# Layer-0 q, k and v projections as reduced-precision matmuls on whole-number weights, with the scales applied to the sums

## The chip, the cores and the metric
One core of one Trainium2 chip runs the kernel. The metric is the device time of one execution in microseconds (us). Engines: PE (TensorE, matmuls), DVE (VectorE), ACT (ScalarE), POOL (GpSimd) and SP (SyncE, here only a queue that issues transfers; ACT and POOL issue transfers too). Each engine and each queue takes its instructions in the order in which the program holds them.

## The reference, cut to what matters
Two transformer layers on 1024 tokens of width 512. The change lies in the attention of layer 0, with 32 query heads and 8 key/value heads of width 128 and 4-bit weights:
```python
w = (qw.astype(jnp.float32) - 8.0) * jnp.repeat(scales, 128, axis=0)   # a scale per 128 rows and column
q, k, v = h @ w_q, h @ w_k, h @ w_v            # h: normalised tokens, 1024 x 512
q, k = q*cos + rotate_half(q)*sin, k*cos + rotate_half(k)*sin
scores = where(causal, q @ k.T / sqrt(128), min)  # 4 query heads share one k and v
ctx = softmax(scores) @ v
x = x + ga * (ctx @ w_o)                       # w_o dequantised like w_q
```
`rotate_half` exchanges the two halves of a head's 128 columns and negates one. A feed-forward layer, a second attention and a second feed-forward layer follow; they are not touched.

## The kernel before
Tokens are held transposed: `hT[half]` has 512 tokens in the free dimension and the 512 features as `NC` = 4 chunks of 128 partitions. A prologue loads, normalises and transposes the tokens and projects the first head group. Then come 8 head groups `g` (one k/v head and its `REP` = 4 query heads each) of 8 steps; a step handles 128 query rows `qi` in the order 3, 7, 2, 6, 1, 5, 0, 4. Steps with `qi` of 4 and more are called long here, the others short. `tc.manual_schedule()` keeps each engine's instructions in the order in which the code writes them, so the loop body is the schedule.

A step works in four slices `s` of 32 query rows (times four heads, so 128 rows of scores):
- `scores(u, s)`: one or two matmuls (L331) into a score tile of two PSUM banks, pool `sp` with three tiles; DVE masks (L335, L337) and takes the maximum (L339); ACT takes the exponential with the row sum (L341) into `pr`.
- `normalize(u, s)`: DVE's reciprocal (L348), ACT's product with it in place (L350).
- `turn_probs(u, b)`: DVE transposes 32x32 blocks (L355), and four transfers (L357) carry the result into `pT`, from SP for even `b` and from POOL for odd `b`. Block 0 is turned at the end of its own step, blocks 1 to 3 in the next.
- `context(old)` (L366): the product of `pT` of two steps ago with v, one matmul for each of its `qi` + 1 blocks, copied out by ACT (L372). `project_o(old)` (L377): four matmuls with the dequantised output weights. `residual`: DVE multiplies by the gate (L385), POOL adds to `x` (L386).

Beside that each step of groups 0 to 6 does some `piece()`s of the next group's projections. `project_rope` runs four float32 matmuls (L219) of 512 columns that accumulate over the chunks in one PSUM bank, DVE multiplies by the cosine (L225) and, half by half with the partitions exchanged, by the sine (L227, L228), and POOL adds both into `kT` or `qT` (L232). `project_v` (L299) does v for two heads in every second group, evicted by `evict` in turn on ACT and DVE. The matmul results of all of these come from one PSUM pool `psA[0]` (tag "mm") of two banks, which `context` and `project_o` use as well. `exchange()` turns weights that have landed into floats (`ready`, DVE's L212; k also by ACT's L276) and loads the next (`load`: the int32 weights and, spread over 128 partitions, their scales). `plan(g, i)` says by hand which weights and pieces belong to which step. The last group has no projections (`last_group_step`).

Of the kernel before, what the change touches and what calls it, by code (L numbers as in the profile page):

```python
# [9 lines left out]
F32 = mybir.dt.float32  # L10
I32 = mybir.dt.int32
# [6 lines left out]
P = 128  # L18
# [24 lines left out]
def block_kernel(ctx: ExitStack, tc: tile.TileContext, a: dict, out: bass.AP):  # L43
# [66 lines left out]
    mod = {}  # L110

# [41 lines left out]
    def gate_row(l, j, bank, spread=None):  # L153

        spread = gate_spread(l, j) if spread is None else spread
        ps = bank()
        for c in range(NC):
            nc.tensor.transpose(ps[:, bass.ts(c, P)], spread[:, c, :], ident)
        g = const.tile([P, D], F32, tag=f"gate{j}", name=f"gate{j}")
        evict(g, ps)  # L160
        mod[l, j] = g
# [25 lines left out]
    with ExitStack() as st:  # L187
        wp = st.enter_context(tc.tile_pool(name="a0w", bufs=3))
        kvp = st.enter_context(tc.tile_pool(name="a0kv", bufs=2))
        rp = st.enter_context(tc.tile_pool(name="a0r", bufs=2))  # L190
        qp = st.enter_context(tc.tile_pool(name="a0q", bufs=2))
        ordered = st.enter_context(tc.manual_schedule())
        psA[0] = st.enter_context(tc.tile_pool(name="psA0", bufs=2, space=PSUM))
        first = st.enter_context(ExitStack())
        fp = first.enter_context(tc.tile_pool(name="m0s", bufs=1))
        tmp_open(first, "m0", bufs=9, wm=4)
        trp = first.enter_context(tc.tile_pool(name="psM0", bufs=4, space=PSUM))
        psA[1] = first.enter_context(tc.tile_pool(name="psM1", bufs=2, space=PSUM))
# [12 lines left out]
        def dequant(dst, q, s):  # L211
            nc.vector.scalar_tensor_tensor(dst, q, -ZERO, s, ALU.add, ALU.mult)  # L212

        def project_rope(dst, wf, halves):

            for half in halves:
                ps = psum_mm()
                for c in range(NC):
                    nc.tensor.matmul(  # L219
                        ps, lhsT=wf[:, c, :], rhs=hT[half][:, c, :],  # L220
                        start=(c == 0), stop=(c == NC - 1),
                    )
                sl = bass.ts(half, 512)
                t1 = rp.tile([P, 512], F32, tag="t1", name="t1")
                nc.vector.tensor_mul(t1, ps, cosT[:, sl])  # L225
                t2 = rp.tile([P, 512], F32, tag="t2", name="t2")
                nc.vector.tensor_mul(t2[0:64, :], ps[64:128, :], sinT[64:128, sl])  # L227
                nc.vector.tensor_mul(t2[64:128, :], ps[0:64, :], sinT[0:64, sl])  # L228
                if len(dst.shape) == 3:
                    t1, t2 = (t.rearrange("p (b i) -> p b i", i=B) for t in (t1, t2))  # L230
                    sl = bass.ts(half, 512 // B)
                nc.gpsimd.tensor_tensor(dst[:, sl], t1, t2, ALU.add)  # L232

        raw, wf = {}, {}
        kT, vv, qT, wo, vs_ = {}, {}, {}, {}, {}

        def load(kind, *n):

            if kind == "m":
                raw[kind, *n] = mod_load(*n)  # L240
                return
            shape = [P, NC, P] if kind in "qk" else [P, 2, 2 * HD] if kind == "v" else [P, D]
            wi = wp.tile(shape, I32, tag="wi", name="wi")
            ws = wp.tile(shape, F32, tag="ws", name="ws")
            if kind in "qk":
                wsrc, ssrc = a[f"qw_{kind}"][n[0]], a[f"s_{kind}"][n[0]]
            elif kind == "v":
                sl = slice(2 * n[1], 2 * n[1] + 2)
                wsrc, ssrc = a["qw_v"][n[0] // 2][:, sl, :], a["s_v"][n[0] // 2][sl, :]
            else:  # L250
                h = n[0] * REP + n[1]
                wsrc, ssrc = a["qw_o"][h * P : (h + 1) * P, :], a["s_o"][h]
            nc.sync.dma_start(wi, wsrc)
            nc.sync.dma_start(ws, ssrc.partition_broadcast(P))
            raw[kind, *n] = wi, ws

        def ready(kind, *n):

            if kind == "m":
                mod_sum(*n, raw.pop((kind, *n)))  # L260
                return
            wi, ws = raw.pop((kind, *n))
            if kind in "qk":
                dst = wp.tile([P, NC, P], F32, tag="wf", name="wf", bufs=2)
                wf[kind, n[0]] = dst
            elif kind == "v":
                if n[1] == 0:
                    vs_[n[0]] = wp.tile([P, NC, 2 * HD], F32, tag="vf", name="vf", bufs=1)
                dst = vs_[n[0]][:, 2 * n[1] : 2 * n[1] + 2, :]
            else:  # L270
                if n[1] == 0:
                    wo[n[0]] = wp.tile([P, REP, D], F32, tag="wo", name="wo", bufs=2)
                dst = wo[n[0]][:, n[1], :]
            dequant(dst, wi, ws)
            if kind == "k":
                nc.scalar.mul(dst, dst, SC0)  # L276

        def project_k(g, half):
            if half == 0:
                kT[g] = kvp.tile([P, S], F32, tag="kT", name="kT")  # L280
            project_rope(kT[g], wf["k", g], (half,))

        def project_q(h, half):

            g, r = divmod(h, REP)
            if (r, half) == (0, 0):
                qT[g] = qp.tile([P, S // B, REP, B], F32, tag="qT", name="qT")
            project_rope(qT[g][:, :, r, :], wf["q", h], (half,))

        def project_v(g, ts):  # L290

            if ts[0] == 0:
                v = kvp.tile([P, NT, 2 * HD], F32, tag="v", name="v")
                vs_[g, "v"] = v
                vv[g], vv[g + 1] = v[:, :, :HD], v[:, :, HD:]
            for t in ts:
                ps = psum_mm()
                for c in range(NC):
                    nc.tensor.matmul(  # L299
                        ps[:, : 2 * HD], lhsT=tok(hT, c, t), rhs=vs_[g][:, c, :],  # L300
                        start=(c == 0), stop=(c == NC - 1),
                    )
                evict(vs_[g, "v"][:, t, :], ps[:, : 2 * HD])
# [84 lines left out]
        def plan(g, i):  # L388


            n, h0 = g + 1, (g + 1) * REP
            if g + 1 == NKV:
                parts = [("m", 1, j, c) for j in (3, 4, 5) for c in range(NC)]
                return parts[2 * i - 2 : 2 * i] if i else [], parts[2 * i : 2 * i + 2], []
            m = (0, 3 + g) if g < 3 else (1, g - 4) if g > 3 else None
            m = [("m", *m, c) for c in range(NC)] if m else []
            v = [("v", n, 0), ("v", n, 1)] if n % 2 == 0 else []
            q = [("q", h0 + r) for r in range(REP)]
            o = [("o", n, r) for r in range(REP)]
            k = [("k", n + 1)] if n + 1 < NKV else []  # L400
            ks = [lambda s=s: project_k(n, s) for s in range(2)]
            qs = [[lambda r=r, s=s: project_q(h0 + r, s) for s in range(2)] for r in range(REP)]
            vp = [lambda t=t: project_v(n, (t, t + 1)) for t in range(0, NT, 2)] if v else []
            if g == 0 and i < 7:
                o0 = [("o", 0, r) for r in range(REP)]
                return (
                    (q[:1], o0[1:2], ks),
                    (q[1:2] + o0[:2], o0[2:] + q[2:3], qs[0]),
                    (o0[2:], q[3:] + o[:1], qs[1]),
                    (q[2:] + o[:1], o[1:], []),  # L410
                    (o[1:], m[:2], qs[2]),
                    (m[:2], m[2:], []),
                    (m[2:], k, qs[3]),
                )[i]
            return (
                ([], o[:1], ks),
                (q[:2], v, []),
                (o[:1] + v, q[2:] + o[1:2], qs[0] + qs[1]),
                (q[2:] + o[1:2], o[2:], []),
                (o[2:], m[:2], qs[2] + vp[:2]),  # L420
                (m[:2], m[2:], []),
                (m[2:], k, qs[3] + vp[2:]),
                (k, [("q", h0 + REP + r) for r in range(2)] if k else [], []),
            )[i]

        hT = [keep.tile([P, NC, 512], F32, tag=f"h{i}", name=f"hT{i}") for i in range(2)]
# [39 lines left out]
        def ln_evict(half, banks):  # L468
            shift, scale1 = mod[0, 0], mod[0, 1]
            for c in range(NC):  # L470
                h = hT[half][:, c, :]
                if c % 2:
                    nc.scalar.activation(
                        h, banks[c], AF.Identity,
                        bias=shift[:, c : c + 1], scale=scale1[:, c : c + 1],
                    )
                else:
                    nc.vector.tensor_scalar(
                        h, banks[c], scale1[:, c : c + 1], shift[:, c : c + 1],
                        ALU.mult, ALU.add,  # L480
                    )
# [27 lines left out]
        ready("k", 0)  # L509
        ln_evict(0, banks)  # L510
        load_tables(0)
        load("v", 0, 0)
        load("v", 0, 1)
# [1062 lines left out]
```

## Time and profile before
| what | value |
|---|---|
| median of 3 timed runs | 1839.43 us (1837.96 to 1839.64) |
| span of the profiled execution | 1835.6 us, 23046 instructions |
| prologue: first L219 matmul to first score matmul | 19.3 to 69.3 us |
| head groups 0 to 6 | 69.3 to 980.0 us |
| last head group | 980.0 to 1095 us |
| everything after layer 0's attention | 1095 to 1835.6 us |
| memory traffic | 74.90 MB read, 2.36 MB written |

The span goes from the first to the last instruction on the chip, the timed runs have a little more around it. Times in views of the trace are microseconds from the span's start. A line such as `L219 PE MATMUL mm<-hT,wf 128*128 128x512 f32 x8` names the line of the kernel, the engine, the operation, the tile written and the tiles read, the shape and how many such instructions were merged; what stands in brackets behind it is the idle time before it and what released it. A float32 matmul leaves two records. Matmuls are pipelined, so that the pitch from start to start says what one costs, not its duration. Line numbers are those of the kernel that a trace or a sentence speaks of.

### The profile page before, as it was taken

What the parts mean: (1) busy time and instruction counts of PE and PEld (TensorE: products, weight loads), DVE (VectorE), ACT (ScalarE), POOL (GpSimd) and SP (SyncE); (2) the same over time, 40 slices, a digit from 0 to 9 for tenths busy, and PEclk for the clock granted to TensorE, in tenths of its full rate; (3) what the DMA queues carried; (4) which work ended last, traced back from release to release, by engine and by line L of the source; (5) the groups of instructions that cost most, each with busy time, mean ns of one, the idle gap of its engine ahead of it and who ended that gap; (6) DMA issues with size and microseconds to landing.
All of it is one profiled execution on the core that took longest, in us unless ns stands there. A gap on an engine that the chain in (4) does not pass through costs nothing.

```text
span 1835.6 us, 23046 instructions
## 1 busy us (share of the span) xinstructions
PE 1786.1 (97%) x6818; PEld 842.1 (46%) x6818; DVE 1164.5 (63%) x2824; ACT 671.4 (37%) x1401; POOL 486.8 (27%) x712
## 2 busy tenths in 40 slices
PE   7999999999999999999999999999999999999999
PEld 4444445444455444455444444444544443333444
DVE  6778675676765777766777764232455678677543
ACT  1143433434434434333345530000114345355631
POOL 1335443444433444434444430001110100200000
PEclk9999999999999999999999999999999999999999
DMA  6164552354543554534544553001000002000000
GB/s 234 57 168 123 133 149 74 105 149 114 137 115 82 127 130 115 149 95 112 122 119 128 149 154 136 1 0 52 1 1 5 8 8 78 4 5 8 8 18 34
DMA packets 87739, 156.40 MB, mean 85 GB/s; under 512 B 25264, under 2 KB 33072, under 8 KB 87616
## 3 DMA queue, kind: packets, MB, share of 16 engines
q1 hardware_dynamic: 70064, 117.00, 22.2%
q0 software_dynamic: 17312, 37.54, 8.5%
q8 instruction: 55, 0.90, 0.2%
q14 instruction: 68, 0.56, 0.1%
q10 hardware_dynamic: 240, 0.41, 0.1%
HBM read 74.90 MB, written 2.36 MB: 42 GB/s over the span
## 4 chain that ended last, share of the span: by engine, by line
PE 73%; DVE 15%; ACT 5%; issue 4%; DMA 2%; SPq 0%; POOL 0%; ACTq 0%; DVEq 0%; POOLq 0%
PE mm L366 10%; PE sc L852 8%; PE sc L331 8%; PE mm L219 8%; PE mm L377 7%; PE sc L1117 6%; PE sc L1070 5%; PE sc L886 4%; PE ctx L1169 4%; DVE pr L355 3%; PE mm L299 3%; PE sc L973 2%; ACT pr L341 2%; ACT pr L350 2%; DVE nb L339 2%
## 5 line engine op out<-in xcount | busy, mean ns | idle before, releaser
L341 ACT ACTIVATE pr<-sc,nb 128x512 f32<-128x512 f32 (+7 forms) x256 | 189.3, 740 | 502.3 <-DVE nb L339 390.6
L219 PE MATMUL mm<-hT,wf 128*128 128x512 f32 x640 | 289.8, 597 | 7.4 <-DVE t L228 3.7
L357 POOL DMA_DIRECT2D pT<-pr x509 | 251.0, 499 | 141.2 <-DMA pT<-pr 41.2
L331 PE MATMUL sc<-kT,qT 128*128 128x512 f32 (+15 forms) x768 | 263.5, 466 | 2.9 <-ACT pr L341 2.9
L366 PE MATMUL mm<-pT,v 128*128 128x512 f32 x576 | 258.7, 594 | 2.0 <-DVE gu L585 1.6
L377 PE MATMUL mm<-wo,ctxT 128*128 128x512 f32 x512 | 232.9, 597 | 7.4 <-DVE wo L212 3.5
L355 DVE STREAM_TRANSPOSE pr<-pr 128x512 f32<-128x512 f32 (+7 forms) x256 | 189.3, 760 | 80.0 <-ACT pr L350 72.5
L331 PEld LDWEIGHTS sc<-kT,qT 128*128 128x128 f32 x768 | 141.9, 191 | 160.2 <-issue 143.6
L1117 PE MATMUL sc<-q,kv 32*128 32x512 f32 (+3 forms) x768 | 194.0, 542 | 3.6 <-DVE mx L1085 2.0
L350 ACT ACTIVATE pr<-pr,rs 128x512 f32<-128x512 f32 (+7 forms) x256 | 190.9, 765 | 8.9 <-DVE rs L348 8.9
L339 DVE TENSOR_REDUCE nb<-sc 128x1 f32<-128x416 f32 (+31 forms) x256 | 181.1, 708 | 8.8
L1133 ACT ACTIVATE pspace<-sc 128x512 f32<-128x512 f32 (+3 forms) x303 | 131.5, 493 | 147.1 <-PE sc L1126 108.1
L219 PEld LDWEIGHTS mm<-hT,wf 128*128 128x128 f32 x640 | 118.4, 190 | 143.7 <-issue 119.1
L1070 PE MATMUL sc<-kv,q 32*128 32x512 f32 (+3 forms) x768 | 174.6, 532 | 3.7 <-DVE mx L1085 1.4
L386 POOL TENSOR_TENSOR x<-x,ot 128x512 f32<-128x512 f32 x62 | 78.4, 1265 | 348.2 <-DVE ot L385 268.5
L366 PEld LDWEIGHTS mm<-pT,v 128*128 128x128 f32 x576 | 107.7, 190 | 121.1 <-issue 113.1
L852 PE MATMUL sc<-hT,gu 128*128 128x512 f32 x352 | 153.3, 594 | 0.9 <-DVE ot L385 0.9
L1080 DVE CUSTOM_DVE_ANT_0 q<-sc,cwide 128x128 f32<-128x128 f32 (+3 forms) x256 | 125.5, 490 | 42.7 <-PE sc L1070 17.6
L377 PEld LDWEIGHTS mm<-wo,ctxT 128*128 128x128 f32 x512 | 96.2, 191 | 115.4 <-issue 100.4
L232 POOL TENSOR_TENSOR qT<-t,t 128x512 f32<-128x512 f32 x64 | 86.5, 1352 | 113.1 <-DVE t L228 112.8
L852 PEld LDWEIGHTS sc<-hT,gu 128*128 128x128 f32 x352 | 66.1, 190 | 86.4 <-issue 81.6
L1117 PEld LDWEIGHTS sc<-q,kv 32*128 32x128 f32 x768 | 71.4, 186 | 71.8 <-ACT pspace L1133 23.3
(199 smaller groups left out, 1849.9 us busy)
## 6 DMA issues: line engine op xcount, KB each, us to landing
wm<-in_wmodT_dram SPq DMA_DIRECT2D x44, 256.0 KB
wi<-in_qw_q_dram SPq DMA_DIRECT2D x32, 256.0 KB
ws<-in_s_q_dram SPq DMA_DIRECT2D x32, 256.0 KB
wi<-in_qw_o_dram SPq DMA_DIRECT2D x32, 256.0 KB
ws<-in_s_o_dram SPq DMA_DIRECT2D x32, 256.0 KB
pT<-pr SPq DMA_DIRECT2D x64, 128.0 KB
pT<-pr POOLq DMA_DIRECT2D x64, 128.0 KB, 3.3
pT<-pr SPq DMA_DIRECT2D x64, 112.0 KB
```

Source lines behind the costliest of these rows:

```text
L219: nc.tensor.matmul(ps, lhsT=wf[:, c, :], rhs=hT[half][:, c, :], start=(c == 0), stop=(c == NC - 1),)
L331: nc.tensor.matmul(ps[:, n0 : n0 + w], lhsT=q, rhs=kT[u.g][:, n0 : n0 + w], start=True, stop=True)
L339: nc.vector.tensor_reduce(nb, ps[:, : d0 + B], AX.X, ALU.max, negate=True)
L341: nc.scalar.activation(u.pr[:, :, :, s, :].rearrange("p j k i -> p k j i"), ps[:, :nk].rearrange("p (k j i) -> p k j i", j=NB, i=B), AF.Ex ...
L350: nc.scalar.activation(pr, pr, AF.Copy, scale=u.rs[s])
L355: nc.vector.transpose(t, t)
L357: queues[(REP * b + r) % len(queues)].dma_start(u.pT[b * B : (b + 1) * B, r, :, :, :].rearrange("p k s i -> p (k s i)"), t[r * B : (r + 1) ...
L366: nc.tensor.matmul(ps, lhsT=vv[u.g][:, kj, :], rhs=u.pT[:, :, kj, :, :], start=(kj == 0), stop=(kj == u.n - 1),)
L377: nc.tensor.matmul(ps, lhsT=u.ctxT[:, r, :], rhs=wo[u.g][:, r, :], start=(r == 0), stop=(r == REP - 1),)
L852: nc.tensor.matmul(ps, lhsT=w[:, m, c, :], rhs=hTc[b][:, c, :], start=(c == 0), stop=(c == NC - 1),)
L1070: nc.tensor.matmul(ps[:, at : at + w], lhsT=u.q[kp, bass.ts(i, P)], rhs=kT1[kp, u.g, n0 : n0 + w], start=True, stop=True,)
L1117: nc.tensor.matmul(ps[:, : QW - q0], lhsT=kT1[kp, u.g, bass.ts(kb, P)], rhs=u.q[kp, q0:QW], start=True, stop=kb < 4 * u.Q,)
```

## The change
The projections of q, k and v are written anew, and the loop around them with it.
- The tokens are kept as two float32r tiles, `hi` (the value as float32r holds it) and `lo` (the rest), made from each transposed bank by one ACT and two DVE instructions.
- Weights of q, k and v become whole numbers in float32r by one ACT instruction (`ready`); their scales are no longer spread over the partitions but stand as one column per head and chunk in `scol`, loaded once. The output weights are dequantised by ACT and POOL.
- One half of one head is a `Job`. `sums`: per chunk two matmuls (`lo`, `hi`) into a bank of its own, so four banks a job; chunks 0 and 2 are evicted with their scale by ACT, chunks 1 and 3 added with theirs by DVE; POOL adds the two partial sums. `swap`: two transfers exchange the halves of the 128 partitions into `r`, on SP (in the prologue on ACT's queue). `end`: POOL multiplies by the cosine (in the prologue DVE), DVE `r` by the sine, POOL adds. For v, `end` transposes on PE and copies out by ACT, so v is projected for one head in every group.
- The PSUM pool of the matmuls has four banks instead of two, that of the score tiles two tiles instead of three.
- In groups 0 to 6 three of four blocks of `turn_probs` go out on SP (`wide`). Short steps open two jobs, long steps one. The hand-written `plan` becomes a table by place, and `exchange` loads whatever fits next.
- `gates[5] = big` places one gate tile in another pool.

```diff
-        psA[0] = st.enter_context(tc.tile_pool(name="psA0", bufs=2, space=PSUM))
+        psA[0] = st.enter_context(tc.tile_pool(name="psA0", bufs=4, space=PSUM))
...
-            dequant(dst, wi, ws)
-            if kind == "k":
-                nc.scalar.mul(dst, dst, SC0)
+                nc.scalar.add(dst, wi, -ZERO)
+                nc.gpsimd.tensor_tensor(dst, dst, ws, ALU.mult)
+                return
...
+            nc.scalar.add(dst, raw.pop((kind, *n)), -ZERO)
+            wf[kind, n[0]] = dst
...
+            def sums(self):
+
+                w, at = wf[self.kind, self.n], place[self.kind] + self.n
+                self.y = y = rp.tile([P, 512], F32, tag="ya", name="ya")
+                z = rp.tile([P, 512], F32, tag="yb", name="yb", bufs=1)
                 for c in range(NC):
-                    nc.tensor.matmul(
-                        ps[:, : 2 * HD], lhsT=tok(hT, c, t), rhs=vs_[g][:, c, :],
-                        start=(c == 0), stop=(c == NC - 1),
+                    ps = psum_mm()
+                    for part in (lo, hi):
+                        nc.tensor.matmul(
+                            ps, lhsT=w[:, c, :], rhs=part[self.half][:, c, :],
+                            start=part is lo, stop=part is hi,
+                        )
+                    dst, s = (y, z)[c // 2], scol[:, at, c : c + 1]
+                    if c % 2 == 0:
+                        nc.scalar.activation(dst, ps, AF.Copy, scale=s)
+                    else:
+                        nc.vector.scalar_tensor_tensor(dst, ps, s, dst, ALU.mult, ALU.add)
+                nc.gpsimd.tensor_tensor(y, y, z, ALU.add)
+
+            def swap(self):
+
+                self.swapped = True
+                if self.kind == "v":
+                    return
+                self.r = rp.tile([P, 512], F32, tag="yr", name="yr")
+                q = nc.scalar if self.early else nc.sync
+                q.dma_start(self.r[0:64, :], self.y[64:128, :])
+                q.dma_start(self.r[64:128, :], self.y[0:64, :])
...
+                first = nc.vector if self.early else nc.gpsimd
+                first.tensor_tensor(y, y, cosT[:, sl], ALU.mult)
+                nc.vector.tensor_mul(self.r, self.r, sinT[:, sl])
+                nc.gpsimd.tensor_tensor(dst, t1, t2, ALU.add)
...
-        sp = st.enter_context(tc.tile_pool(name="a0s", bufs=3, space=PSUM))
+        sp = st.enter_context(tc.tile_pool(name="a0s", bufs=2, space=PSUM))
...
+        wide = [nc.sync] * 3 * REP + [nc.gpsimd] * REP
...
                 scores(u, 0)
...
+                turn_prev(1)
+                close_job()
+                if qi < NT // 2:
+                    open_job()
+                    scores(u, 1)
+                    turn_prev(2)
+                    normalize(u, 0)
+                    turn_prev(3)
+                    swap()
                     if old:
                         context(old)
+                    scores(u, 2)
+                    normalize(u, 1)
+                    close_job()
+                    open_job()
+                    scores(u, 3)
+                    normalize(u, 2)
+                    exchange(g, i)
+                    swap()
+                else:
+                    scores(u, 1)
...
+                    normalize(u, 0)
+                    turn_prev(2)
+                    turn_prev(3)
+                    open_job()
+                    if old:
+                        context(old)
+                    swap()
+                    scores(u, 2)
+                    normalize(u, 1)
+                    exchange(g, i)
+                    scores(u, 3)
+                    normalize(u, 2)
+                    close_job()
+                assert not waiting
                 if old:
                     ps = project_o(old)
+                normalize(u, 3)
...
+                for b in range(2 if (g, i) == (NKV - 2, NT - 1) else 1):
+                    turn_probs(u, b, wide)
                 if old:
                     residual(old, ps)
```
`open_job` starts the next waiting job, `swap` issues the transfers of the oldest job that has none yet, `close_job` ends the oldest job that has been swapped.

## The prediction
> **What bounds the kernel now.** I read the page first: TensorE (PE) is the only engine near its limit.
> ```profile
> PE 1786.1 (97%) x6818; PEld 842.1 (46%) x6818; DVE 1164.5 (63%) x2824; ACT 671.4 (37%) x1401; POOL 486.8 (27%) x712
> ```
> Then busy time by stretch, cut where the first score matmul of each head group starts. Columns: length, then busy time of PE, weight load, DVE, ACT, POOL, then granted clock and DMA.
> ```profile
> 593.30:717.00 123.70, 122.94 (x313) 57.50 (x312) 89.11 (x207) 52.28 (x107) 54.89 (x82) 1.00 0.49 124
> 717.00:856.10 139.10, 137.07 (x378) 69.39 (x377) 93.49 (x213) 53.74 (x111) 54.88 (x82) 1.00 0.44 118
> ```
> PE has under 2.1 us idle in a group. Groups that also project v take 139.1, the others 123.7; the six full ones average 131.5. DVE is already at two thirds. From 1095 us on nothing changes.
>
> Third, one long step (group 5, qi 7), engine by engine, since the change moves work from PE to DVE, ACT, POOL and the queues. PE, each record half of one float32 matmul:
> ```profile
> 731.39 3.33 PE L331 MATMUL sc<-kT,qT 128*128 128x512 f32 x8
> 734.55 4.46 PE L366 MATMUL mm<-pT,v 128*128 128x512 f32 x10
> 738.85 3.54 PE L331 MATMUL sc<-kT,qT 128*128 128x512 f32 x8
> 742.23 3.60 PE L377 MATMUL mm<-wo,ctxT 128*128 128x512 f32 x8
> ```
> Start to start: five context matmuls take 4.30 (0.86 each), two score slices 3.38, the output projection 3.43. DVE of that step, with its end:
> ```profile
> 733.67 0.14 DVE L335 MEMSET sc<- 128x96 f32 x1
> ...
> 735.12 0.70 DVE L355 STREAM_TRANSPOSE pr<-pr 128x512 f32<-128x512 f32 x1
> ...
> 747.84 1.25 DVE L355 STREAM_TRANSPOSE pr<-pr 128x1024 f32<-128x1024 f32 x1 [1.91 <-ACT pr L350]
> 749.01 0.65 DVE L385 TENSOR_TENSOR ot<-mm,gate 128x512 f32<-128x512 f32 x1
> 749.68 0.14 DVE L335 MEMSET sc<- 128x96 f32 x1
> ```
> One slice costs DVE 1.45 (memset, mask, max). DVE starts the step's first slice 2.3 us after PE began it, and the next step's 4.0 after (749.68 against 745.66). DVE's round is 16.0 us where PE's is 14.3: already longer, and only PE's long projections let DVE catch up. ACT:
> ```profile
> 742.40 1.11 ACT L341 ACTIVATE pr<-sc,nb 128x1024 f32<-128x1024 f32 x1 [2.22 <-PE sc L331]
> ...
> 743.50 1.14 ACT L350 ACTIVATE pr<-pr,rs 128x1024 f32<-128x1024 f32 x1
> 744.54 1.10 ACT L341 ACTIVATE pr<-sc,nb 128x1024 f32<-128x1024 f32 x1
> ```
> An exponential with its read-back takes 1.10, a normalisation 1.04.
>
> **What PE is spared.** A q or k half costs 4 x 0.86 = 3.45, a v head the same. A job is now 8 float32r matmuls of 512 columns, of which the trace has none. The nearest row is v's, whose records also last half of a 512-column record's pitch:
> ```profile
> 22.81 7.07 PE L299 MATMUL mm<-vf,hT 128*128 128x256 f32 x32
> ```
> 29.71 - 22.81 over 32 is 0.216 us each. Bounds: 0.129 (bf16, 128 columns: 33.0 us over 256) and 0.43 (a whole float32 record). I take 0.216, so 1.73 per job. The Trainium skill, FP8 and Floating Point Precision, TensorE Precision Notes, gives four passes for float32 and truncation to a shorter format for the reduced read; one pass of four would make a job 1.72. No run so far shows it. Per group: minus 11 x 3.45, plus 12 x 1.73, plus 8 transposes at 0.11: 131.5 becomes 115.2. If PE stayed the bound, 7 x 16.3 = 114 us would be gained.
>
> **Where it goes instead.** The matmul banks are now a ring of four, and one job fills all four. In a long step PE's order is score slices 0 and 1, the job, context. The context takes the bank of the job's first chunk, so it waits for ACT's scaled eviction of that chunk (`sums`), and ACT's order puts that behind exponential 1 and normalisation 0. In the program of after this wait stands on the first context matmul of every long step. So DVE's round becomes one serial chain. Long step qi 7: slice 0 1.45, transpose 0.71, the sine product of the job before 0.69 (as L225 and L227), slice 1 1.45, exp 1.10, normalise 1.04, eviction 0.65 (between 0.58 of the context copy L372 and 0.77 of L473), context 4.30, score slice 2 1.69, its DVE part 1.45, exp 1.10, normalise 1.04, ACT's dequantisation 0.63 (L276), exp 1.10, two normalisations 2.08, transpose 1.17, residual product 0.67; six crossings between engines 0.5. Sum 22.8. The same with the shorter rows and other contexts: qi 6 25.0 (context of 8 blocks, three dequantisations), qi 5 22.0, qi 4 20.2; together 90.0.
>
> Short step qi 3: slice 0 0.9; the first two chunks wait for exp 0.68 and eviction 0.65: 2.3; two DVE evictions 1.37, slice 1 0.9, two transposes and a reciprocal 1.8: 6.4. Meanwhile the SyncE queue, which now carries 12 probability transfers a step instead of 8, and at 0.63 us each, sends four after the second transpose (5.4 to 7.95), then the two swaps behind them (to 9.2). This row, of the same size, is 3.3 from POOL:
> ```profile
> pT<-pr POOLq DMA_DIRECT2D x64, 128.0 KB, 3.3
> ```
> From SyncE I read 2.4 in the semaphores: landing at 11.0. DVE stands at the sine product until then, and behind it are the next job's evictions, slice 3's mask and max, and so ACT's exponential 3: 0.7 + 1.37 + 0.9 + 0.8 + 1.3 + 0.7 + 0.67. Sum 17.5. qi 2 16.7, qi 0 14.8, qi 1 (v, no swap) 14.3; together 63.3.
>
> A group is then 153.3 instead of 131.5: 7 x 21.8 = +153. DVE's busy work hardly changes: three rope products of 0.69 and a dequantisation of 0.66 give way to two evictions and one product. POOL loses half of its transfers (16 us a group) and gains about 35 of products and sums; it has the room.
>
> The gap on PE has a price of its own. This one, in group 0,
> ```profile
> 115.05 3.78 PE L377 MATMUL mm<-wo,ctxT 128*128 128x512 f32 x4 [3.51 <-DVE wo L212]
> ```
> brought this:
> ```profile
> 113.57:120.40 6.83, 5.35 (x7) 2.25 (x8) 3.37 (x7) 1.79 (x4) 1.64 (x2) 0.50 0.99 224
> ```
> 6.83 us at half clock, 3.4 us of work late. A long step of after leaves PE idle from 5.1 (slices 3.38, job 1.73) to DVE's lag of 4 plus 7.1, about 6 us, and the context that follows is on the chain. Bounds 0 and 3.4 per long step; I take 2: 28 x 2 = +56.
>
> The prologue (19.3 to 69.3, PE-bound) becomes DVE's: 10 early jobs x 2.72 + 2 x 1.34, 10.9 for the two-part tokens, 8 for statistics, norm and gate sums, 49 in all, with waits for swaps and POOL: between -5 and +15, I take +5. The last group has no projections but score banks fall from three to two, and its PE waits for ACT already (1.54 at 984.77): 0 to 2 us in each of 8 steps, +8. Weight and scale loads shrink; the queue that carries them is in the chain above.
>
> One rule speaks against the change and is outside the sum. The Trainium skill, SBUF — State Buffer, SBUF: two separate sides, makes a DVE instruction with two SBUF inputs and a GpSimd instruction exclude each other. DVE's rope products read PSUM before; the sine product reads SBUF twice, so it could wait for a POOL product. No row shows this; by the rule and L386's 1.27 it would be an estimated 0.2 to 1.3 us in 70 products, 14 to 90 us more.
>
> The sum: the profiled execution is 1835.6 of span and 3.8 outside it against the median 1839.4. 1839.4 + 153 + 56 + 5 + 8 = 2061 us.
>
> **Rivals.** (a) PE stays the bound: 1839.4 - 114 + 13 = 1738. For it: ACT busy 42% in a group, DVE's sum unchanged. Against it: it needs the context's bank free when the job ends, that is lag + 7.1 at most 5.1, so DVE ahead of PE, which no step of before shows. 11%. (b) The chain is shorter: no clock loss, and swaps landed before DVE asks (2.2 us less in three short steps): 146.7 a group, 1839.4 + 106 + 13 = 1958; with less lag still, down to 1845. 22%. (c) The change doesn't deliver: float32r at 0.43 makes PE's group 136; the chain does not contain the job's length, so 2061 hardly moves, and only under (b) would it show, 1839.4 + 32 + 13 = 1884. Inside (b), 4%. The forecast's own case, 1960 to 2170, has 64%; beyond that 2%; no change 1%.
>
> **The numbers.** A measurement tells about 0.2% (3.7 us) from no change. Faster 0.11, same 0.01, slower 0.88. From 1880 to 2170 the range leaves out (a), no change, the mildest 5% of (b), and what lies above: 2 in 10.
>
> **What would show it.** Right: idle time before L406 released by ACT's evictions in long steps, groups of about 150 us or more, PE under 85% there, a granted clock of 0.5 in pieces, DVE waiting for the swap at L324. Wrong at step one: float32r pitch far from 0.216. Wrong altogether: context starting right after the job, groups near 115.

## The result, and the profile after

| | before | after |
|---|---|---|
| median of 4 runs each, us | 1839.5 (1838.0 to 1840.9) | 2196.5 (2194.4 to 2197.6) |
| span of the profiled execution | 1835.6 | 2195.8 |
| prologue, up to the first score matmul | 69.3 | 94.1 |
| head groups 0 to 6 | 910.7 | 1211.3 |
| last group's first score matmul to the end | 855.6 | 890.4 |

The ratio is 1.194 (1.192 to 1.195). The three stages add 24.8, 300.6 and 34.8 us, together the 360.2 by which the span grew. The direction was forecast; the time lies 26 us above the range.

First the engines' row of the page after, then the stage of groups 0 to 6 (length, then busy time of PE, weight load, DVE, ACT and POOL, granted clock, DMA share, GB/s):
```profile
PE 1802.4 (82%) x6754; PEld 871.6 (40%) x6754; DVE 1160.7 (53%) x2782; ACT 833.4 (38%) x1670; POOL 646.3 (29%) x686
94.10:1305.40 1211.30, 901.91 (x2329) 458.30 (x2330) 620.69 (x1415) 513.72 (x987) 524.28 (x530) 0.88 0.38 97
```
No engine is near its limit: PE is busy for three quarters of the groups' time, DVE for half. The matmuls became fewer, and yet PE is busy longer (1802 against 1786), in the main because the granted clock fell to 0.88 in the groups.

PE in a long step (group 2, qi 7), from its job to its context, and ACT meanwhile:
```profile
464.80 0.39 PE L277 MATMUL mm<-hi,wf 128*128 128x512 f32 x1
465.03 0.39 PE L277 MATMUL mm<-lo,wf 128*128 128x512 f32 x1
...
473.00 7.01 PE L406 MATMUL mm<-pT,v 128*128 128x512 f32 x10 [6.42 <-ACT ya L283]
479.84 2.68 PE L371 MATMUL sc<-kT,qT 128*128 128x512 f32 x6
```
```profile
470.12 1.11 ACT L381 ACTIVATE pr<-sc,nb 128x1024 f32<-128x1024 f32 x1 [1.95 <-DVE rs L388]
...
471.23 1.14 ACT L390 ACTIVATE pr<-pr,rs 128x1024 f32<-128x1024 f32 x1
472.27 0.68 ACT L283 ACTIVATE ya<-mm,scol 128x512 f32<-128x512 f32 x1
```
A float32r matmul of 512 columns has a pitch of 0.23 us: the promised saving is there. But the context waits 6.42 us for ACT's eviction (L283) of the job's first chunk, which stands on ACT behind exponential 1 and normalisation 0, and then runs partly at half clock (granted 0.64 over these 6.84 us): 6.84 us start to start for five matmuls that took 4.30 before.

The waits of the whole run, PE's and DVE's (total, times, longest):
```profile
PE mm L406 <- ACT ya L283: 155.5, 52, 9.1
PE sc L371 <- ACT pr L381: 73.0, 31, 6.0
PE mm L277 <- DVE ot L425: 67.0, 29, 3.2
```
```profile
DVE sc L375 <- PE sc L371: 237.3, 56, 10.2
DVE yr L324 <- DMA yr<-ya: 133.9, 33, 6.9
DVE ya L285 <- ACT ya L283: 89.8, 71, 2.2
```
Four things are to be told apart: the context's bank (155.5), the swap (133.9), the other waits that the four evictions of a job bring (89.8, and 67.0 where the fourth chunk waits for the bank of the last output projection, which DVE still reads), and the score tiles (73.0). DVE's largest wait, 237.3 for a score slice, is mostly for the slices that PE reaches only behind the late context: it falls to 36.6 in e1 below, where the context goes first.

### The profile page after: what moved, and what is told of

Its sections match the earlier page's. It is cut to its first block, busy times and chain, and to the rows that moved or that the text cites. A ratio compares the mean times of both kernels' runs of the same rounds, so it can differ in the third digit from the quotient of the medians.

```text
span 2195.8 us, 23626 instructions
## 1 busy us (share of the span) xinstructions
PE 1802.4 (82%) x6754; PEld 871.6 (40%) x6754; DVE 1160.7 (53%) x2782; ACT 833.4 (38%) x1670; POOL 646.3 (29%) x686
## 3 DMA queue, kind: packets, MB, share of 16 engines
q1 hardware_dynamic: 85248, 139.40, 23.1%
## 4 chain that ended last, share of the span: by engine, by line
PE 54%; DVE 16%; ACT 10%; DMA 8%; issue 6%; SPq 3%; POOL 2%; ACTq 0%; DVEq 0%; POOLq 0%
PE mm L406 12%; PE sc L908 7%; DMA yr<-ya 6%; PE sc L371 5%; PE sc L1173 5%; PE sc L1126 4%; PE mm L417 4%; ACT pr L390 4%; PE sc L942 4%; DVE nb L379 4%; PE ctx L1225 3%; DVE pr L395 3%; ACT pr L381 3%; SPq L397 2%; PE sc L1029 2%
## 5 line engine op out<-in xcount | busy, mean ns | idle before, releaser
L406 PE MATMUL mm<-pT,v 128*128 128x512 f32 x576 | 340.0, 746 | 157.4 <-ACT ya L283 155.5
L371 PE MATMUL sc<-kT,qT 128*128 128x512 f32 (+15 forms) x768 | 288.7, 494 | 74.7 <-ACT pr L381 73.0
L277 PE MATMUL mm<-lo,wf 128*128 128x512 f32 x384 | 190.6, 496 | 112.7 <-DVE ot L425 67.0
L406 PEld LDWEIGHTS mm<-pT,v 128*128 128x128 f32 x576 | 132.8, 241 | 337.1 <-ACT ya L283 183.6
L397 POOL DMA_DIRECT2D pT<-pr x285 | 142.6, 506 | 147.4 <-DVE pr L395 31.5
L286 POOL TENSOR_TENSOR ya<-ya,yb 128x512 f32<-128x512 f32 x96 | 127.9, 1332 | 152.4 <-DVE yb L285 147.4
L277 PE MATMUL mm<-hi,wf 128*128 128x512 f32 x384 | 166.0, 432 | 0.0
L908 PE MATMUL sc<-hT,gu 128*128 128x512 f32 x352 | 153.3, 594 | 0.9 <-DVE ot L425 0.9
L375 DVE MEMSET sc<- 128x96 f32 (+2 forms) x192 | 21.4, 112 | 239.2 <-PE sc L371 237.3
L277 PEld LDWEIGHTS mm<-lo,wf 128*128 128x128 f32 x384 | 80.4, 209 | 163.3 <-DVE ot L425 80.1
L323 POOL TENSOR_TENSOR ya<-ya,cosT 128x512 f32<-128x512 f32 x70 | 106.2, 1517 | 130.2 <-DMA yr<-ya 130.2
```

The source lines that it names most:

```text
L277: nc.tensor.matmul(ps, lhsT=w[:, c, :], rhs=part[self.half][:, c, :], start=part is lo, stop=part is hi,)
L371: nc.tensor.matmul(ps[:, n0 : n0 + w], lhsT=q, rhs=kT[u.g][:, n0 : n0 + w], start=True, stop=True)
L397: queues[(REP * b + r) % len(queues)].dma_start(u.pT[b * B : (b + 1) * B, r, :, :, :].rearrange("p k s i -> p (k s i)"), t[r * B : (r + 1) ...
L406: nc.tensor.matmul(ps, lhsT=vv[u.g][:, kj, :], rhs=u.pT[:, :, kj, :, :], start=(kj == 0), stop=(kj == u.n - 1),)
L908: nc.tensor.matmul(ps, lhsT=w[:, m, c, :], rhs=hTc[b][:, c, :], start=(c == 0), stop=(c == NC - 1),)
```

## The experiments

Every kernel is read by the same three stages. "Rest" is from the last group's first score matmul to the end. Before, after, e4, e7, e12 and e13 were timed four times and more, the others once; four executions of one kernel lay 3 to 11 us apart, so that 10 us between single executions is not much.

| kernel | us | prologue | groups 0 to 6 | rest |
|---|---|---|---|---|
| before | 1839.5 | 69.3 | 910.7 | 855.6 |
| after | 2196.5 | 94.1 | 1211.3 | 890.4 |
| e1_ctx_first | 2038.2 | 94.7 | 1050.0 | 891.7 |
| e11_noswap | 1946.1 | 94.7 | 958.6 | 890.3 |
| e9_one_bank | 1918.4 | 81.3 | 944.3 | 891.0 |
| e15_one_bank_ctx_noswap | 1811.5 | 80.6 | 841.4 | 887.7 |
| e2_swap_pool | 2206.1 | 95.0 | 1217.0 | 891.5 |
| e5_queues | 2048.3 | 94.5 | 1059.6 | 892.2 |
| e3_before_banks | 1868.8 | 71.4 | 900.4 | 895.2 |
| e6_ends | 2164.1 | 93.9 | 1211.9 | 856.3 |
| e10_ya4 | 2181.4 | 77.4 | 1210.9 | 891.3 |
| e8_all | 1992.2 | 94.6 | 1037.5 | 858.2 |
| e4_f32r_only | 1792.0 | 55.5 | 875.4 | 858.7 |
| e7_single | 1790.7 | 56.4 | 875.3 | 857.5 |
| e12_deq | 1794.1 | 57.7 | 882.0 | 857.4 |
| e13_deq_banks | 1803.3 | 57.9 | 890.2 | 855.5 |

### Groups 0 to 6: three causes, taken away one after the other

**e1_ctx_first**
```diff
-                    open_job()
                     if old:
                         context(old)
+                    open_job()
                     swap()
```


> The kernel after, with one swap of lines: in long steps context(old) is issued ahead of the job instead of behind it, so that the context's bank no longer waits for ACT's eviction of the job's first chunk. Theory (the bank ring with ACT's order stops PE, and the half clock follows from those gaps): the 155 us of PE idle time before the context matmuls fall to under 40, a long step shortens by 3.5 to 5 us, and the time goes from 2196.5 to between 2060 and 2110 us. Rival (the DVE-ACT-POOL round of a step is as long anyway, through shared SBUF ports and swaps): the idle time moves to the job's fourth chunk or to the next scores, and the time stays above 2165 us.

Measured 2038.2: 158 us less, 22 us beyond the theory's range; groups 0 to 6 alone lost 161. PE's wait before L406 fell from 155.5 to 18.5, and DVE's for the score slices with it:
```profile
PE mm L406 <- ACT ya L283: 18.5, 20, 4.7
```
```profile
DVE sc L375 <- PE sc L371: 36.6, 48, 2.8
```
So the bank wait, with the half clock that follows it, is worth 161 us.

**e11_noswap**: e1 without the transfers.
```diff
-                q.dma_start(self.r[0:64, :], self.y[64:128, :])
-                q.dma_start(self.r[64:128, :], self.y[0:64, :])
+                if self.early:
+                    q.dma_start(self.r[0:64, :], self.y[64:128, :])
+                    q.dma_start(self.r[64:128, :], self.y[0:64, :])
...
+                if not self.early:
+                    nc.vector.tensor_mul(self.r, y, sinT[:, sl])
...
-                nc.vector.tensor_mul(self.r, self.r, sinT[:, sl])
+                if self.early:
+                    nc.vector.tensor_mul(self.r, self.r, sinT[:, sl])
```


> e1_ctx_first, with no swap transfers in groups 0 to 6: DVE multiplies the sum itself by the sine. Part of the computation is left out: the exchange of the halves. e2 and e5 moved these transfers or what stands before them to other queues, and the time rose by 10 us each time; this takes the transfer and its landing away altogether. Theory (the landing is part of the chain, wherever it is issued): DVE's 163 us of idle time before the sine product go, half of that shows, 1930 to 1985 us. Rival (slack: the fourth chunk's bank, held by the output projection until the residual product, and ACT's evictions end as late): above 2020 us.

Measured 1946.1, as the theory had it: another 91 us of the groups. DVE's wait for the landing is gone there; its wait for ACT's evictions has grown from 123.6 us in e1 to 164.1.

**e9_one_bank** and **e15_one_bank_ctx_noswap**: e9 is the kernel after with one bank per job; e15 has e1's and e11's edits as well.
```diff
-                z = rp.tile([P, 512], F32, tag="yb", name="yb", bufs=1)
+                ps = psum_mm()
                 for c in range(NC):
-                    ps = psum_mm()
                     for part in (lo, hi):
...
-                            start=part is lo, stop=part is hi,
+                            start=(c == 0 and part is lo), stop=(c == NC - 1 and part is hi),
...
-                nc.gpsimd.tensor_tensor(y, y, z, ALU.add)
+                nc.scalar.activation(y, ps, AF.Copy, scale=scol[:, at, 0:1])
```


> The kernel after, with each job's eight matmuls accumulating in one bank, evicted by one ACT instruction; DVE's two scaled additions and POOL's sum are gone, copies, queues, score tiles and order stay. Part of the computation is changed: only the first chunk's scales are applied, to the whole sum. Theory (the four banks of a job and the five evictions behind them are the cause of the 300 us in groups 0 to 6): a group takes 123 to 140 us, the prologue ends below 80, the last group stays near 147; 1850 to 1935 us. Rival (swaps by copies and the queue they stand in cost as much): groups above 152 us, above 2030 us in all.

> e9_one_bank with the context ahead of the job in long steps and no swap transfers in groups 0 to 6, so that all three suspects are out while the two score tiles, the twelve transfers on SP and the weights by ACT and POOL stay. Part of the computation is changed: one chunk's scales on the whole sum, halves not exchanged. Theory (these three are the whole loss, and the matmuls' gain then shows): a group takes 116 to 127 us, groups 0 to 6 come to 815 to 890 us, below the 911 of before; 1790 to 1870 us in all. Rival (score tiles, SP's queue or ACT's weights hold the groups too): a group stays at 131 or more, above 1895 us.

Both came out inside the theories' totals: e9 1918.4 with groups of 134.9 on average, e15 1811.5 with groups of 120.2 (e9's prologue of 81.3 is 1.3 above its figure). This is e15's stage, to be read against that of after above:
```profile
80.60:922.00 841.40, 784.42 (x2329) 423.84 (x2330) 500.74 (x1245) 460.46 (x902) 399.07 (x445) 0.99 0.46 118
```
The same 2329 PE instructions take 784 us of busy time instead of 902. Most of these 117.5 us are the clock: after spent some 290 us of its groups at half clock (twice 0.12 of 1211.3), PE was busy for 209 of them, and at full clock half of that would have done, an estimate of 105 us; for e15 the same reckoning gives 6. And with the same two score tiles, the same twelve transfers on SP and the same weights by ACT and POOL the groups are 69 us below those of before. So the matmuls' gain exists, and three things buried it: context behind the job 161 us, swaps 91, sums in four banks 117 (958.6 to 841.4). The last figure takes the banks together with what reads them, four evictions and POOL's sum, without which DVE's busy time in the groups falls from 623 us in e11 to 501; no run parts the two. The split depends on the order in which they are taken out (e9 alone gives back 267, since one bank per job also frees the context's bank); the sum of 370 does not.

### The queue theory, which fell

**e2_swap_pool** changes one word, **e5_queues** two in e1:
```diff
-                q = nc.scalar if self.early else nc.sync
+                q = nc.scalar if self.early else nc.gpsimd
```
```diff
-                turn_prev = lambda b: prev and turn_probs(prev, b, wide)
+                turn_prev = lambda b: prev and turn_probs(prev, b, queues)
...
-                    turn_probs(u, b, wide)
+                    turn_probs(u, b, queues)
```


> The kernel after, with the two swap transfers of each job in groups 0 to 6 issued by POOL instead of SP. Theory (the swaps come late because twelve probability transfers and the weight loads stand ahead of them on SP, and DVE waits for them at the sine product): DVE's 134 us of idle time before the sine product fall to under 50 and the time falls by 40 to 80 us, to between 2115 and 2155 us. Rival (that wait is slack, the bank ring sets the step): less than 15 us faster, above 2180 us.

> e1_ctx_first, with the probability transfers of groups 0 to 6 alternating between SP and POOL block by block as in the kernel before (eight a step on SP, eight on POOL) instead of twelve on SP. Theory (with the bank wait gone, the swap behind twelve transfers on SP is next: in e1 the swap of a short step went out at 752.78 though its data were there at 749.56, and DVE stood still for 5.46): DVE's idle time before the sine product, 163 us in e1, falls below 110 and the time falls from 2038 to between 1975 and 2015 us. Rival (the sine product waits anyway, for POOL's sum): above 2028 us.

Both are misses: no faster but 10 us slower, in one execution each, and DVE's wait before the sine product stayed (166 us in e5 against 163 in e1). In the kernel after the swap does stand behind twelve transfers:
```profile
577.00 7.82 SPq L397 DMA_DIRECT2D pT<-pr  x12
584.92 0.54 SPq L295 DMA_DIRECT2D yr<-ya  x1
```
On POOL in e2 it stands behind that engine's own four; here is POOL, then DVE, at the same step:
```profile
582.93 1.27 POOL L286 TENSOR_TENSOR ya<-ya,yb 128x512 f32<-128x512 f32 x1 [1.86 <-DVE yb L285]
585.93 2.01 POOL L397 DMA_DIRECT2D pT<-pr  x4 [1.74 <-ACT ctxT L412]
...
588.45 0.54 POOL L296 DMA_DIRECT2D yr<-ya  x1
```
```profile
592.31 0.69 DVE L324 TENSOR_TENSOR yr<-yr,sinT 128x512 f32<-128x512 f32 x1 [5.92 <-DMA yr<-ya]
```
From the end of the issue to the sine product 3.3 us pass, from DVE's last addition (582.85) 9.5. The price of the swap is this path of sum, queue, issue and landing, whichever of the two queues it takes; of the runs only e11, which leaves it out, gives time back. None issued the swap ahead of the probability transfers: in e2 3.7 us of the 9.5 lie between the end of POOL's sum (584.20) and the first of the two issues (587.93).

### The two ends

**e3_before_banks** is the kernel before with the PSUM split of after; **e6_ends** the kernel after with the last group's split of before and the prologue's swaps on SP; **e10_ya4** the kernel after with two more buffers for `y` in the prologue.
```diff
-        psA[0] = st.enter_context(tc.tile_pool(name="psA0", bufs=2, space=PSUM))
+        psA[0] = st.enter_context(tc.tile_pool(name="psA0", bufs=4, space=PSUM))
...
-        sp = st.enter_context(tc.tile_pool(name="a0s", bufs=3, space=PSUM))
+        sp = st.enter_context(tc.tile_pool(name="a0s", bufs=2, space=PSUM))
```
```diff
-                q = nc.scalar if self.early else nc.sync
+                q = nc.sync
...
+            if g + 1 == NKV:
+                mid.close()
+                del psA[1]
+                sp = st.enter_context(tc.tile_pool(name="a0t", bufs=3, space=PSUM))
```
```diff
-                self.y = y = rp.tile([P, 512], F32, tag="ya", name="ya")
+                if self.early:
+                    self.y = y = fp.tile([P, 512], F32, tag="ye", name="ya", bufs=4)
+                else:
+                    self.y = y = rp.tile([P, 512], F32, tag="ya", name="ya")
```


> The kernel before, with the PSUM split of the kernel after: four banks for the matmuls, two score tiles. Nothing else differs, so this prices the third score tile alone. Theory (the last group's +32 us come from the lost score tile): the last group goes from 115.5 to 140 to 150 us, the groups before it lose little because projections cover the wait (0 to 30 us over seven groups), 1865 to 1900 us in all. Rival (my forecast's term, +8 in the last group, nothing elsewhere, and the +32 of after come from something else): 1840 to 1852 us.

> The kernel after, with two edits in stages that do not touch each other. One: the prologue's swaps go out on SP instead of ACT's queue. Theory: in the prologue of after a swap stands on ACT's queue behind an eviction that itself waits for POOL's sum of the job before last (the buffer ya), so each q or k job takes about 6.1 us; on SP, idle there, the prologue's end falls from 94.1 to between 72 and 84 us. Rival (DVE's work sets the prologue): above 90. Two: the last group gets three score tiles and two matmul banks back. Theory: it returns from 147.6 us to within 4 of the 115.5 of before. Groups 0 to 6 unchanged, 1211. Together 2140 to 2155 us.

> The kernel after, with four buffers instead of two for the sum y of the prologue's jobs. Theory (in the prologue ACT's first eviction of a job waits for POOL's last sum of the job before last, which holds y: a ring of ACT 0.7, DVE's two additions 1.4, the two rope products 1.3 to 2.4, POOL 1.3, about 6.1 us for each q or k job): the prologue ends at 72 to 84 us instead of 94.1, everything else unchanged, 2174 to 2187 us. Rival (DVE's own work, 49 us by my forecast, and its waits within a job set it): above 90 us, time unchanged.

The third score tile explains the rest stage from both sides: taken from the kernel before it costs 39.6 us there (e3), given back to the kernel after it restores 856.3 against 855.6 (e6). In e3 slice 2 of the last group's qi 7 waits for exponential 0 to leave its tile:
```profile
987.99 1.26 PE L330 MATMUL sc<-kT,qT 128*128 128x512 f32 x2 [4.23 <-ACT pr L340]
```
Groups 0 to 6 came out 10 us shorter in e3, with two banks more and one score tile less: there the projections cover the score tile's wait.

The prologue's first theory fell: with the swaps on SP it ended at 93.9 instead of 94.1. The second held, 77.4. The chain is that of the buffer: ACT's first eviction of a job waits for POOL's last sum of the job before last, here twice in the kernel after, 6.07 us apart:
```profile
51.67 0.69 ACT L283 ACTIVATE ya<-mm,scol 128x512 f32<-128x512 f32 x1 [6.49 <-POOL qT L325]
...
57.74 0.69 ACT L283 ACTIVATE ya<-mm,scol 128x512 f32<-128x512 f32 x1 [4.81 <-POOL qT L325]
```
Why the earlier swap of e6 bought nothing, DVE and POOL of e6 show:
```profile
54.10 1.77 DVE L325 TENSOR_TENSOR yr<-yr,sinT 128x512 f32<-128x512 f32 x1
```
```profile
53.73 1.59 POOL L287 TENSOR_TENSOR ya<-ya,yb 128x512 f32<-128x512 f32 x1 [2.31 <-DVE yb L286]
```
The data had landed, but the sine product fell beside POOL's sum and took 1.77 us instead of its usual 0.68. Of the prologue's 24.8 us the buffer ring is 16.7; the other 8 were not followed further.

### All four waits at once

**e8_all** has the edits of e1, e5 and e6 and moves the jobs: in a long step behind score slice 2, in a short step the first job is closed after the second is opened.


> The change with its four waits taken out together: context ahead of the job and the job behind score slice 2 in long steps, the first job of a short step closed after the second is opened, probability transfers alternating between SP and POOL, prologue swaps on SP, three score tiles in the last group. The arithmetic is that of the kernel after. Theory (the 357 us come from waits, not from the engines' work): 1870 to 1950 us. Rival (the work itself, with shared SBUF ports, keeps a group at 145 us or more): above 1980 us.

A miss: 1992.2, groups of 148.2, which is where the rival put them. The ends came as in e6. The rival's reason is not what the trace shows: of the groups' 1037 us PE was busy for 867, DVE for 632, POOL for 647. The waits only changed hands. PE and DVE of e8:
```profile
PE mm L278 <- DVE ot L426: 89.6, 26, 4.3
```
```profile
DVE yr L325 <- DMA yr<-ya: 131.8, 53, 6.3
```
A job needs all four banks of the ring, while the context or the output projection holds one of them until ACT or DVE comes round to it. Another order chooses who waits. It does not make a fifth bank. e8 is the fastest version with the whole arithmetic of the change, and 153 us above the kernel before.

### The faster matmuls alone

**e4_f32r_only** is the kernel before with two float32r matmuls for each float32 one; **e7_single** has one. This is the whole of e7:
```diff
-                dst = wp.tile([P, NC, P], F32, tag="wf", name="wf", bufs=2)
+                dst = wp.tile([P, NC, P], F32R, tag="wf", name="wf", bufs=2)
...
-                    vs_[n[0]] = wp.tile([P, NC, 2 * HD], F32, tag="vf", name="vf", bufs=1)
+                    vs_[n[0]] = wp.tile([P, NC, 2 * HD], F32R, tag="vf", name="vf", bufs=1)
...
-        hT = [keep.tile([P, NC, 512], F32, tag=f"h{i}", name=f"hT{i}") for i in range(2)]
+        hT = [keep.tile([P, NC, 512], F32R, tag=f"h{i}", name=f"hT{i}") for i in range(2)]
```


> The kernel before with its own schedule, banks and rope, but the projections' four float32 matmuls per half head as eight float32r matmuls that accumulate in one bank. Part of the computation is changed: the weights keep their scales and are rounded to float32r, the two parts are the same rounded tokens, halved. So this is the price of the matmuls alone: at 0.23 us each a half head takes 1.84 instead of 3.45, a group's PE work falls from 131.5 to about 112. Theory (DVE's round of about 16 us in a long step is the next bound): groups of 122 to 128, 1775 to 1815 us. Rival (PE stays the bound): groups near 113, about 1705 us. Rival (no gain, DVE is as late already): above 1830 us.

> The kernel before with nothing changed but the type of the projections' tokens and weights, float32r instead of float32: one pass of four matmuls at 0.23 us in place of four at 0.86. Part of the computation is changed: tokens and weights, scales included, are rounded to float32r. Theory (e4's groups were no longer bound by PE but by DVE's round, so the second halving of the projections' PE time buys little): groups of 115 to 123 on average, 1750 to 1785 us. Rival (PE was still the bound in e4): another 11 x 0.92 = 10 us a group less, about 1715 us.

Both are faster than either kernel: ratios to before 0.975 (0.972 to 0.978) and 0.973 (0.970 to 0.976). They lie together: halving the projections' PE work once more bought nothing in the groups (875.4 and 875.3). So PE's work no longer sets the time; e7 lies 6 us above even its theory's range. This is what PE does in e7 in the jobs of a short step (group 5, qi 2):
```profile
713.17 1.20 PE L220 MATMUL mm<-hT,wf 128*128 128x512 f32 x4 [2.06 <-DVE ot L386]
...
717.19 3.70 PE L367 MATMUL mm<-pT,v 128*128 128x512 f32 x8 [2.23 <-DVE t L229]
...
725.10 1.19 PE L220 MATMUL mm<-hT,wf 128*128 128x512 f32 x4 [2.00 <-ACT ctxT L373]
```
With two banks PE waits each time until one has been read out: by DVE the output projection (L386) or a projection of q (L229), by ACT the context (L373).

**e12_deq** takes the weights' 0.66 us off DVE, **e13_deq_banks** adds two banks:
```diff
-            dequant(dst, wi, ws)
+            nc.scalar.add(dst, wi, -ZERO)
+            nc.gpsimd.tensor_tensor(dst, dst, ws, ALU.mult)
```


> e7_single, with the weights turned into numbers by ACT (minus eight) and POOL (times scale), as the kernel after does it, instead of one DVE instruction of 0.66 us. Theory (e4 and e7 take the same time because DVE's round, not PE, bounds them): 9 to 11 DVE instructions less in a group make it 3 to 7 us shorter, 1743 to 1772 us. Rival (DVE's round is bound by waits for ACT's exponentials, and ACT's extra 0.62 us each lie in that same round): no change or slower, 1785 us or more.

> e12_deq with four matmul banks and two score tiles in groups 0 to 6, and two banks and three tiles in the last group. In e3 this split made groups 0 to 6 10 us faster in all and cost its time in the last group only. Theory (PE's waits for banks that DVE's rope still reads, 50 us in e7, go): 10 to 35 us faster than e12_deq. Rival (with shorter projections the second score tile is missed in the groups as it is in the last one): slower than e12_deq by 10 us or more.

Neither helped: 1794.1, ratio 0.975 (0.973 to 0.977), which is the rival's case, and 1803.3, ratio 0.980 (0.979 to 0.982), near its rival's: there PE waits 73 us for score tiles instead. DVE's busy time in the groups fell from 637 us in e7 to 591 in e12 for no gain, so its amount of work is not the limit either. What is left, by these waits, is the round between PE, DVE and ACT in which one waits for another's bank or tile; no run shows that directly. e7 and e4, the same within their spread, are the fastest versions that ran; of e7's 49 us against before 35 lie in the groups and 13 in the prologue. e7 keeps less of the operands than the kernel after: tokens and weights are rounded to float32r.

## Why the prediction was right or wrong

- **What PE is spared.** Right: pitch 0.23, not the 0.43 of rival (c). The sum has a slip: a v head costs two halves, not one, since the row shown, 6.9 us, is half the tokens of two heads. Twelve times 3.45 taken off instead of eleven makes a PE-bound group 111.7, not 115.2. e15's groups of 120.2, with PE busy for 112, come near it.
- **The context behind the job.** Right, place and releaser as named. PE's share in the groups, 74%, is under the 85% that was to show it.
- **A group of 153.3.** Too short, and this is the step that failed most: with its clock term it was 161.3, the run has 173.0 on average, 92 us over the seven groups. The forecast's steps are DVE's rounds, from one step's first mask (L375) to the next one's. In group 2 the long steps qi 7, 6, 5, 4 took 25.8, 28.0, 23.1 and 23.3, where 24.8, 27.0, 24.0 and 22.2 stood with their 2 us of clock: 100.2 against 98.0. The short ones qi 3, 2, 1, 0 took 18.6, 18.9, 16.4 and 19.9 against 17.5, 16.7, 14.3 and 14.8: 73.8 against 63.3. So the chain of the long steps was about right, and the short steps were mis-sized. This is qi 0 on DVE:
```profile
577.53 0.14 DVE L375 MEMSET sc<- 128x96 f32 x1
...
589.46 0.69 DVE L324 TENSOR_TENSOR yr<-yr,sinT 128x512 f32<-128x512 f32 x1 [5.71 <-DMA yr<-ya]
...
597.40 0.14 DVE L375 MEMSET sc<- 128x96 f32 x1
```
Its sine product waited 5.71 us for its swap, and a gate's sums, 4.1 us (591.89 to 595.95), came behind it. For qi 0 the prediction gives its total alone, so which of its terms was short stays open; the one short step whose sum is written out, qi 3, has no gate's sums. DVE then began qi 4 8.8 us after PE (588.63), where I had given every long step a lag of 4: from PE's first score matmul to its next qi 4 takes 28.3 us. In qi 1 I left out the output projection as a user of the ring. The job's fourth chunk stood 3.20 us for its bank, and the context behind it ran at half clock, 5.28 us for three matmuls, 2.58 by the 0.86 of before, while DVE waited 2.11 us for the slice behind that; I had put half clock into long steps only.
- **Half clock, +56.** Not settled: PE's busy time in the groups holds about 105 us of it by the estimate above, and how much of that moved the end no run separates.
- **Waiting for swaps.** Right as an effect. The reason that the prediction's step gave, four more transfers ahead of it on SP, was not what set it (e2, e5); rival (b), swaps landed before DVE asks, did not come: DVE waited for 33 of them, 4 us each.
- **Prologue, +5.** Wrong: 24.8. I added up DVE's work (49 us) and did not ask who holds `y`. A ring of two buffers through ACT, DVE and POOL was in the code to be read, and costs 16.7 (e10).
- **Last group, +8.** Wrong: 34.8. The 1.54 us that PE waited for ACT with three tiles was taken for the size of the wait with two. e3 prices the tile at 39.6.
- **The port rule outside the sum.** The Trainium skill, SBUF — State Buffer, SBUF: two separate sides, has a DVE instruction with two SBUF inputs and a GpSimd instruction lock each other out. The 1.77 beside 0.68 in e6 agrees. In the groups of the kernel after, though, it was not the sine product that was held, as the 14 to 90 us had it: it took 0.71 on average. POOL's cosine product just behind it took 1.52 against 1.27 alone: 0.25 over 70 products is 18 us of POOL's time, and no run shows how much of it moved the end.

Of the 135 us between 2061 and 2196.5 the groups make 92, the last group 27 and the prologue 20 (the spans differ by 3 us more than the medians). The direction came from the named mechanism, not from luck. What the two ends took beyond their own upper bounds, 59.6 us against 31 (+15, and 2 in each of 8 steps), is more than the 26 us beyond the range, though the prediction does not derive its 2170 from its terms.

## What to carry to other kernels

When a sum that accumulated in one PSUM bank is taken apart so that each part can be scaled, count bank by bank who reads it and what stands before that reader in its engine's order; here PE's saving was worth nothing because the next matmul needed one of those banks. Price a faster form of an instruction by itself first: here a change of three types, with nothing else moved, gave 49 us, and the structure built around the same instruction cost 357. Buffers, score tiles and banks that a change takes are terms of the sum even in stages that the change does not touch.

## What the runs showed of the hardware that I had not expected

PE's clock halved without any long gap. These are windows of e7 at the lines shown above; the last is a half-clock piece:
```profile
712.91:716.33 3.42, 1.79 (x6) 1.05 (x6) 3.32 (x7) 0.67 (x2) 1.82 (x3) 1.00 0.67 155
...
723.16:726.57 3.41, 1.47 (x6) 1.06 (x7) 3.35 (x7) 1.65 (x4) 2.65 (x5) 1.00 0.60 154
726.57:729.98 3.41, 3.41 (x6) 1.33 (x5) 3.36 (x7) 0.81 (x3) 0.71 (x1) 0.50 0.75 198
```
No gap there was over 2.23 us. After a window with 1.47 of 3.41 us busy the clock was 0.50 for the next; after one with 1.79 of 3.42 it stayed full. Over the groups of three runs, cut into such windows, the highest busy share that was followed by half clock was 48% in e7, 49% in after and 52% in e13, the lowest that was followed by full clock 46%, 44% and 47%. By the granted clock e7 spent some 80 us of its groups at half clock, e4, with twice the matmuls in its projections, 14; that may be part of why less PE work bought no time, but no run separates it. The Trainium skill, TensorE: Matmul & The Clock Gate, What's actually happening, gives half clock after an idle window of about 3.4 us; the length of the pieces agrees, but a window busy for 43% was enough here.

A very short DVE instruction can be held too: in the kernel after one of 128x4 took 1.12 us beside a sum of POOL (592.58 to 594.31), where it takes 0.17 alone.
```profile
84.67 0.17 DVE L143 TENSOR_SCALAR sgn<-mcol 128x4 f32<-128x4 f32 x1
...
593.21 1.12 DVE L143 TENSOR_SCALAR sgn<-mcol 128x4 f32<-128x4 f32 x1
```
